# Inverse norms of a two-layer attention block by logarithm, exponential and a Newton step, with a newly searched order of operations

## The chip, the cores and the metric

The kernel runs on one core of one Trainium2 chip. The metric is the device time of one execution in microseconds. Five engines work side by side: TensorE (PE in the profile, its weight loads PEld), VectorE (DVE), ScalarE (ACT), GpSimd (POOL), and SyncE (SP), which here only issues DMAs.

## The reference

Everything is in float32. The input x has 4 sequences of 1024 positions with 256 features. It is normalized (layer norm), and two branches work on the result; their sum and x are the output.

```
xn  = layernorm(x)
out = x + first(xn) + layers(xn)

first(xn):                         # one attention, 16 heads of 64
    h = rms_norm(xn) * gamma
    q, k, v = h @ W_qkv            # window of 64 keys back
    o = softmax(mask(q k^T / 8)) v
    return (o * sigmoid(h @ W_gates + b_gates)) @ W_out

layers(x), twice:                  # 8 heads of 64
    h = shift_token(x)             # half of the features from the position before
    q, k, v = h @ wqkv
    q = q / |q| * q_scale          # l2norm per head
    k = k / |k| * k_scale
    q, k = rotary_xpos(q, k)       # cos, sin and a scale by position
    o = softmax(mask(8 q k^T)) v   # window of 128 keys back
    x = x + o @ wo
    h = layernorm(shift_token(x)) * ln_g + ln_b
    a, g = split(h @ w1 + b1)
    x = x + (a * gelu(g)) @ w2 + b2
```

## The kernel before

The 4096 positions are worked off in 16 blocks of 256 (`TB`), each in two halves of 128 positions (`NT` = 2), one position to a partition. For each block there are three passes: `first_attention`, and `layer` for layers 0 and 1 with `after_attention` behind it (the part from the residual to the gated feed-forward). The first attention of all blocks comes first, and layer 0 starts while its last blocks are still being worked on (`MIX` = 3). A layer's `after_attention` for a block is written down up to two blocks later (`LAG` = 2).

The code does not issue these steps directly. Each step becomes an `Op` of a `Plan`, with the engines that may do it, an estimated duration on each, the buffers it reads and writes, and, for ScalarE, a mode ("exp" or "gelu"; a change of mode makes ScalarE load another table). `Plan.run` then plays the whole program through in time while the kernel is being built. Whenever an engine is free it takes the waiting operation with the lowest score:

```
score = o.due + self.IDLE * (t - at[e]) + (self.TURN[e] if turn else 0.0)
if o.dense and row - self.REFILL * (t - at[e]) + o.dense > self.ROW:
    score += self.CROWD
```

Here `due` is when the operation is due for TensorE's sake, `IDLE` is the price of leaving the engine idle, `TURN` the price of a change of mode, and `CROWD` a price for standing many small matmuls close together. `DEAR` weighs an engine against another where an operation has a choice. `spare` says how many buffers of each kind are held back. The outcome is one list, `plan.order`; `emit` issues it in that order, so each engine's queue and the DMA queues of SP follow it.

TensorE works in two modes: "full" (128x128 weights) for projections, feed-forward and transposes, and "rc" (64x64 weights, four places of the array) for attention scores and sums. Lines that matter below: 791 (first attention's queries and keys), 702 (its values), 825 and 917 (its scores and sums), 952 (its output projection), 1009 (a layer's query, key and value projection), 1150 (its scores), 1242 (its attention sums), 1267 (its output projection), 1437 (the feed-forward's first product, "up"), 1483 and 1497 (its second, "down" and its rest). Line 431 is ScalarE's half of `move`, which copies PSUM to SBUF (or SBUF to SBUF); 433 is VectorE's. Line 500 is the transpose of 32x32 blocks on VectorE behind a DMA round trip through DRAM; 483 and 492 are the DMAs of that round trip.

The place of the change is in `layer`. For each half block, `sq` (line 1043, ScalarE) squares queries and keys, `ss` (line 1050, VectorE) sums them over each head into 16 numbers per position, and `norms` (lines 1056 to 1058, GpSimd) makes the inverse square roots: a maximum with 1e-24, `rsqrt` (line 422, an element-wise power of −0.5 with a tile of exponents, `mhalf`), and a change of sign for the 8 query heads. There are 64 such half blocks (2 layers, 16 blocks, 2 halves). The key half of the result scales the rotated keys (`kn`, line 1119) before they are transposed; the query half comes in later, as a factor in the masked minimum over the scores (`least`, line 1171), whose sign makes the largest score the least. The exponential of line 1185 follows, then the reciprocal of the sums (line 1197) and the weighing on GpSimd (line 1205). Rotation is `rot` (line 1077, GpSimd), `cos` (1093, VectorE) and `add` (1101, either). `rsqrt` is used too for the first attention's statistics and for the layer norm in `after_attention` (`deviation`, lines 1355 to 1366). The gelu is line 1451, its product with the other half lines 1462 and 1467.

Of the kernel before, what the change touches and what calls it, by code (L numbers as in the profile page):

```python
# [8 lines left out]
AF = mybir.ActivationFunctionType  # L9
ALU = mybir.AluOpType  # L10
# [3 lines left out]
P = 128  # L14
# [17 lines left out]
HB = 8  # L32
# [15 lines left out]
LAG = 2  # L48
MIX = 3
BOTH = False  # L50

# [6 lines left out]

# [9 lines left out]
class Op:  # L71
    __slots__ = (
        "us", "fn", "bufs", "mode", "out", "rank", "lat", "left", "ready", "users", "done",
        "start", "end", "eng", "name", "n", "due", "dense",
    )


class Plan:
    LAT = {"PE": 0.25, "DVE": 0.20000000000000004, "ACT": 0.20000000000000004, "POOL": 0.20000000000000004, "SP": 2.0}
    SLACK = {"DVE": 1.1, "POOL": 1.05, "ACT": 1.15}  # L80
    SWITCH = {"PE": 0.1, "ACT": 1.4}
    TURN = {"PE": 10.0, "ACT": 60.0}
    IDLE = 200.0
    LOOK = 150.0
    ROW, REFILL = 640, 300.0
    CROWD = 60.0
    DEAR = {"DVE": 3.0}

# [8 lines left out]

    def op(self, us, fn, r=(), w=(), a=(), mode=None, out=None, lat=None, name="", dense=0):


        o = Op()
        o.us, o.fn, o.mode, o.lat, o.name = us, fn, mode, lat, name
        o.dense = dense
        o.out = out or mode
# [3 lines left out]
        o.users, o.done, o.ready = [], False, 0.0  # L108
        deps = set()
        for b in r:  # L110
# [18 lines left out]
    def run(self):  # L129
        engines = ("PE", "ACT", "DVE", "POOL", "SP")  # L130
        at = dict.fromkeys(engines, 0.0)
        mode = dict.fromkeys(engines)
# [7 lines left out]
        for o in reversed(self.ops):  # L140
            took = min(o.us.values()) + (0.5 if o.lat is None else o.lat)
            o.due = min([o.rank, *(u.due - took for u in o.users)])
        for o in self.ops:
            if not o.left:
                enter(o)
        oldest, out, row = 0, [], 0
# [17 lines left out]
        while len(out) < len(self.ops):  # L164
# [57 lines left out]
            for u in o.users:  # L222
                u.ready = max(u.ready, give)
                u.left -= 1
                if not u.left:
                    enter(u)
            out.append(o)
        self.order = out

    def emit(self):  # L230
        for o in self.order:
            o.fn(o.eng)


@with_exitstack
def layers_kernel(
# [41 lines left out]
        },  # L278
        {"w": (3, 0.05, 20), "g": (1, 0.0, 1), "s": (4, 0.05, 12), "ps": (0, 0.02, 3), "d": (1, 0.0, 1)},
    )  # L280
# [3 lines left out]
    def fixed(shape, name):  # L284
        return Buf(None, const.tile(shape, F32, name=name))
# [87 lines left out]
    load(mask_a.t, mask_a_d, mask_a, eng="ACT")  # L373
    mhalf = fixed([P, 2 * HB], "mhalf")
    op({"POOL": 0.1}, lambda e: nc.gpsimd.memset(mhalf.t, -0.5), w=(mhalf,))
# [39 lines left out]
    def by_feature(b, i, near=False):  # L415


        of = "p (c i a r) -> p i c a r" if near else "p (a c i r) -> p i c a r"
        return b.t[:, : NT * DIM].rearrange(of, a=4, c=NC, i=NT)[:, i]

    def rsqrt(dst, src):
        nc.gpsimd.tensor_tensor(dst, src, mhalf.t[:, : src.shape[1]], ALU.pow)  # L422
# [543 lines left out]
    def layer(l, n, before):  # L966
# [33 lines left out]
        for i in range(NT):  # L1000
# [38 lines left out]
            for m in range(2):  # L1039
# [14 lines left out]
                )  # L1054
            def norms(e, nrm=nrm, rn=rn):
                nc.gpsimd.tensor_scalar_max(nrm.t[:, : 2 * HB], nrm.t[:, : 2 * HB], 1e-24)
                rsqrt(rn.t[:, : 2 * HB], nrm.t[:, : 2 * HB])
                nc.gpsimd.tensor_scalar_mul(rn.t[:, :HB], rn.t[:, :HB], -1.0)

            op({"POOL": 3.5}, norms, r=(mhalf,), w=(nrm, rn), name="rn")  # L1060
            qT = buf("w")
# [497 lines left out]
    plan.run()  # L1559
    plan.emit()  # L1560

def _constants():
# [5 lines left out]
    def half_tiles():  # L1570


        c, r = np.arange(WB)[None, :], p % D
        at = (c >= r) & (c <= r + P)
        first = at & (c >= np.where(p >= D, D, P))
        return np.where(np.stack([at, first], 1), f(0), f(-1e30)).astype(f)

# [15 lines left out]
    cos, sin = np.cos(freqs), np.sin(freqs)  # L1593
    ways = (scale * f(8), f(1) / scale)

# [44 lines left out]
```

## Time and profile before

| | |
|---|---|
| times of three runs | 1695.48, 1693.13, 1694.20 us; median 1694.2 us |
| the profiled execution | 1694.2 us, span 1694.2 us |
| granted TensorE clock | 1.000 |
| busy, share of the span | PE 99%, VectorE 76%, GpSimd 70%, ScalarE 66% |
| instructions | 48683 |
| DMA | 353 MB, mean 208 GB/s |

Busy time is the union of an engine's instructions. Matmuls are pipelined and the profile models their ends, so a busy TensorE need not be at its peak. The page also cuts the span into 40 slices with the busy share in tenths, follows back the chain of work that ended last, and lists groups of instructions by line: busy time, mean duration in ns, idle time of the engine just before them, and what ended it. The list of waits says who waited for whom: total, times, longest.

### The profile page before, as it was taken

The numbers are of one execution on the slowest core, as the hardware profiler recorded it, in microseconds if no ns is written. First come the engines' busy times: TensorE is split into PE (matmuls) and PEld (weight loads), VectorE is DVE, ScalarE is ACT, GpSimd is POOL, SyncE is SP. The second block draws the span as 40 slices with busy tenths as digits, with TensorE's granted clock in tenths as the row PEclk, the third lists the DMA queues.
The fourth block names the chain that finished last, engine by engine and source line by source line (L and its number), as shares of the span: only waits on it lengthen the run. The fifth ranks groups of instructions, "written<-read, shape, count | busy, mean of one in ns | idle before, by whom it ended". The sixth has DMA issues, their size and how long they took to land.

```text
span 1694.2 us, 48683 instructions
## 1 busy us (share of the span) xinstructions
PE 1669.5 (99%) x16454; PEld 1269.0 (75%) x16454; DVE 1288.3 (76%) x4508; ACT 1121.9 (66%) x3417; POOL 1192.5 (70%) x2013
## 2 busy tenths in 40 slices
PE   9999999999999999999999999999999999999998
PEld 7888888888877767777777776677667767777777
DVE  5665655655657788888888878888899888888863
ACT  4665675656657776776676667766677677667763
POOL 4663654644467889888788779887798688887840
PEclk9999999999999999999999999999999999999999
DMA  7885776866567887877778887887778867777760
GB/s 222 237 233 155 224 213 193 228 175 182 167 169 218 227 232 225 222 204 221 215 200 239 236 221 208 248 238 202 201 217 238 242 198 212 213 222 216 203 197 22
DMA packets 487383, 353.16 MB, mean 208 GB/s; under 512 B 167639, under 2 KB 424542, under 8 KB 487134
## 3 DMA queue, kind: packets, MB, share of 16 engines
q1 hardware_dynamic: 486430, 349.86, 72.7%
q8 instruction: 129, 2.11, 0.5%
q14 instruction: 120, 0.98, 0.2%
q10 hardware_dynamic: 704, 0.21, 0.1%
HBM read 168.29 MB, written 143.92 MB: 184 GB/s over the span
## 4 chain that ended last, share of the span: by engine, by line
PE 53%; POOL 3%; DVE 1%; ACT 1%; issue 1%; DMA 1%; SPq 0%; POOLq 0%; DVEq 0%; ACTq 0%
PE ps L1437 17%; PE ps L1009 14%; PE ps L1483 7%; PE ps L1267 6%; PE ps L1242 4%; PE ps L1150 4%; POOL w L1077 1%; PE ps L1497 1%; POOL s L422 1%; POOL w L1205 1%; ACT w L431 1%; DMA w<-d 0%; DMA out_dram<-w 0%; POOL w L1101 0%; DMA sc<-in_L_ffn_k_scale_dram 0%
## 5 line engine op out<-in xcount | busy, mean ns | idle before, releaser
L431 ACT COPY w<-ps 128x512 f32<-128x512 f32 (+3 forms) x624 | 327.7, 585 | 329.7 <-PE ps L791 96.3
L500 DVE STREAM_TRANSPOSE w<-w 128x256 f32<-128x256 f32 (+2 forms) x781 | 450.5, 621 | 95.7 <-DMA w<-d 35.8
L1009 PE MATMUL ps<-w,w 128*128 128x512 f32 x768 | 347.6, 595 | 1.7 <-DVE w L1467 0.7
L880 POOL TENSOR_SCALAR w<-w,s,s 128x128 f32<-128x128 f32 x512 | 227.5, 462 | 146.1 <-DVE s L870 114.0
L1437 PE MATMUL ps<-w,w 128*128 128x256 f32 (+1 forms) x1452 | 312.0, 373 | 1.1 <-ACT w L431 1.1
L1437 PEld LDWEIGHTS ps<-w,w 128*128 128x128 f32 x1452 | 268.3, 190 | 45.5 <-issue 5.9
L1205 POOL TENSOR_SCALAR w<-w,s 128x192 f32<-128x192 f32 (+1 forms) x512 | 230.7, 471 | 91.8 <-DVE s L1197 85.7
L422 POOL TENSOR_TENSOR s<-s,mhalf 128x16 f32<-128x16 f32 (+3 forms) x113 | 228.9, 2025 | 62.7 <-DVE s L643 32.6
L1185 ACT ACTIVATE w<-w,s 128x192 f32<-128x192 f32 (+1 forms) x512 | 223.0, 439 | 48.1 <-DVE w L500 11.2
L1009 PEld LDWEIGHTS ps<-w,w 128*128 128x128 f32 x768 | 144.3, 190 | 147.3 <-issue 127.0
L1077 POOL TENSOR_TENSOR w<-w,w 128x256 f32<-128x256 f32 x256 | 198.2, 780 | 58.9 <-ACT w L431 38.8
L791 PE MATMUL ps<-w,w 128*128 128x256 f32 x1024 | 230.3, 381 | 2.9 <-ACT w L431 1.7
L791 PEld LDWEIGHTS ps<-w,w 128*128 128x128 f32 x1024 | 193.0, 190 | 37.1 <-ACT w L431 3.9
L861 ACT ACTIVATE w<-w,s 128x128 f32<-128x128 f32 x512 | 197.4, 390 | 23.8 <-DVE s L851 11.6
L1171 DVE CUSTOM_DVE_ANT_0 w<-ps,mask_b,s 128x192 f32<-128x192 f32 (+1 forms) x512 | 177.9, 402 | 15.4 <-PE ps L1150 4.9
L1483 PE MATMUL ps<-w,w 128*128 128x256 f32 x640 | 144.8, 380 | 3.6 <-DVE w L1462 3.3
L1093 DVE TENSOR_TENSOR w<-w,w 128x256 f32<-128x256 f32 x256 | 125.8, 537 | 27.4 <-ACT w L431 21.1
L1483 PEld LDWEIGHTS ps<-w,w 128*128 128x128 f32 x640 | 120.9, 190 | 30.7 <-issue 9.9
L1451 ACT ACTIVATE g<-ps,b 128x256 f32<-128x256 f32 (+1 forms) x198 | 86.4, 467 | 84.8 <-PE ps L1437 82.0
L851 DVE CUSTOM_DVE_ANT_0 w<-ps,mask_a 128x128 f32<-128x128 f32 x512 | 111.8, 284 | 28.9 <-PE ps L825 24.4
L1267 PE MATMUL ps<-w,w 128*128 128x256 f32 x512 | 126.6, 390 | 6.7 <-ACT w L431 3.1
L1267 PEld LDWEIGHTS ps<-w,w 128*128 128x128 f32 x512 | 92.7, 189 | 35.7 <-ACT w L431 15.7
(87 smaller groups left out, 2471.2 us busy)
## 6 DMA issues: line engine op xcount, KB each, us to landing
d<-w SPq DMA_DIRECT2D x301, 256.0 KB
w<-d SPq DMA_DIRECT2D x301, 256.0 KB
d<-w SPq DMA_DIRECT2D x224, 192.0 KB
w<-d SPq DMA_DIRECT2D x224, 192.0 KB
w<-w SPq DMA_DIRECT2D x256, 128.0 KB
w<-c SPq DMA_DIRECT2D x81, 256.0 KB
c<-w SPq DMA_DIRECT2D x48, 256.0 KB
w<-in_L_attn_x_dram SPq DMA_DIRECT2D x16, 256.0 KB
```

Of the source, the lines that this page charges most:

```text
L422: nc.gpsimd.tensor_tensor(dst, src, mhalf.t[:, : src.shape[1]], ALU.pow)
L431: nc.scalar.copy(dst(), src())
L500: lambda e, b=b, to=to, at=at, k=k: nc.vector.transpose(to(b), v3(t, 4, m, 32)[:, :, at : at + k]),
L791: nc.tensor.matmul(pq.t[:, j * TB : (j + 1) * TB], W[c].t[:, p % GA * P : (p % GA + 1) * P], hT.t[:, c * TB : (c + 1) * TB], start=(c == 0 ...
L880: nc.gpsimd.tensor_scalar(run(s, u), run(s, u), sm.t[:, at : at + 1], gate.t[:, h : h + 1], ALU.mult, ALU.mult,)
L1009: nc.tensor.matmul(p.t, y.t[:, at : at + P], w["wqkv"][m][c].t[:, :512], start=(c == 0), stop=(c == NC - 1),)
L1077: nc.gpsimd.tensor_tensor(rot.t[:, :512].rearrange("p (h u k r) -> p u k h r", h=2, u=2, k=PB)[:, u], raw[m].t[:, :512].rearrange("p (k h ...
L1185: nc.scalar.activation(v2(ex, 2, (3 - k0) * D)[:, u].rearrange("p (a k r) -> p k a r", k=3 - k0, a=2), v2(s, 2, WB)[:, u, k0 * D :].rearra ...
L1205: nc.gpsimd.tensor_scalar(v2(ex, 2, m)[:, u], v2(ex, 2, m)[:, u], sm.t[:, at : at + 1], 1.0, ALU.mult, ALU.mult,)
L1267: nc.tensor.matmul(pw.t[:, :DIM], v3(oT, 2, 2, P)[:, p % 2, p // 2], v2(w["wo"][p // 2], 2, DIM)[:, p % 2, :], start=(p == 0), stop=(p == ...
L1437: nc.tensor.matmul(pf.t[:, n_ * TB : (n_ + 1) * TB][:, cols], wt, d.t[:, c * TB : (c + 1) * TB][:, cols], start=(c == 0), stop=(c == NC - 1),)
L1483: nc.tensor.matmul(pz.t[:, :DIM], gT[m // 2].t[:, at : at + P], v2(w["w2"][m // 2], 2, DIM)[:, m % 2, :], start=(m == 0), stop=False,)
```

## The change

Three things change. The norms of the layers leave GpSimd's power: the sums are clamped on VectorE or GpSimd, ScalarE takes their logarithm and the exponential of −0.5 times it, and VectorE or GpSimd refines this with one Newton step. The sign of the queries moves into the rotation tables, and that of the mask with it. And the order is another: the planner's prices have other values, 28 ranges of operations have their due times shifted by pseudo-random amounts (`NUDGES`), a matmul operation that follows another on TensorE counts as ready when that one ends, and the table that has both logarithm and exponential is loaded by name whenever ScalarE turns to "exp".

```diff
+NUDGES = [
+    (3500828213, 6053, 6213, 26), (962684833, 7739, 7818, 42), (972045936, 7349, 7406, 6),
+    (83998847, 153, 210, 5), (76883089, 7565, 7620, 20), (3275595751, 4672, 4864, 6),
+    (438986454, 7689, 7721, 90), (1531916726, 5229, 5323, 9), (3939820594, 7664, 7861, 21),
+    (3050749052, 2441, 2480, 24), (971591458, 4443, 4747, 4), (2170321430, 4709, 4906, 24),
+    (3913640632, 4835, 4963, 4), (842596981, 2642, 2828, 12), (814815308, 5466, 5547, 25),
+    (2025033581, 2674, 2735, 11), (352340027, 7429, 7565, 6), (1888537629, 7649, 7682, 18),
+    (3075992983, 7680, 7721, 91), (951854742, 6717, 6777, 9), (159045329, 7340, 7419, 34),
+    (2211461150, 2597, 2649, 15), (1845618598, 3431, 3526, 5), (763246061, 6898, 6987, 12),
+    (3348864259, 7298, 7342, 4), (200214347, 5984, 6059, 6), (1383019642, 2231, 2285, 19),
+    (318795953, 2687, 2722, 9),
+]
+HASTE = 1.2477144070116626
...
+def part(seed, i):
+    x = (seed * 2654435761 + i * 2246822519) & 0xFFFFFFFF
+    x = (x ^ x >> 15) * 2654435761 & 0xFFFFFFFF
+    return (x ^ x >> 13) / 4294967296.0 - 0.5
...
-    TURN = {"PE": 10.0, "ACT": 60.0}
-    IDLE = 200.0
-    LOOK = 150.0
+    TURN = {"PE": 7.841459753622532, "ACT": 17.36077070419636}
+    IDLE = 251.92185968639595
+    LOOK = 158.7882403426324
     ROW, REFILL = 640, 300.0
-    CROWD = 60.0
-    DEAR = {"DVE": 3.0}
+    CROWD = 17.03349668372114
+    DEAR = {"DVE": 1.9317326986533034}
...
+        sway = [0.0] * len(self.ops)
+        for seed, lo, hi, by in NUDGES:
+            for i in range(lo, hi):
+                sway[i] += by * part(seed, i)
         for o in self.ops:
+            o.due = o.due - o.hurry * HASTE + sway[o.n]
...
-                u.ready = max(u.ready, give)
+                u.ready = max(u.ready, o.end if e == "PE" and "PE" in u.us else give)
...
-    def emit(self):
+    def emit(self, load_exp):
+        mode = None
         for o in self.order:
+            if o.eng == "ACT" and o.mode:
+                if o.mode == "exp" and mode != "exp":
+                    load_exp()
+                mode = o.mode
             o.fn(o.eng)
...
-        {"w": (3, 0.05, 20), "g": (1, 0.0, 1), "s": (4, 0.05, 12), "ps": (0, 0.02, 3), "d": (1, 0.0, 1)},
+        {"w": (0.0, 0.07702659706019774, 35.46116717265452), "g": (1.0, 0.0, 1.0), "s": (4.0, 0.05, 12.0), "ps": (0.0, 0.02268601358766725, 3.0), "d": (1.0, 0.0, 1.0)},
...
-    mhalf = fixed([P, 2 * HB], "mhalf")
+    mhalf = fixed([P, 4], "mhalf")
...
-            def norms(e, nrm=nrm, rn=rn):
-                nc.gpsimd.tensor_scalar_max(nrm.t[:, : 2 * HB], nrm.t[:, : 2 * HB], 1e-24)
-                rsqrt(rn.t[:, : 2 * HB], nrm.t[:, : 2 * HB])
-                nc.gpsimd.tensor_scalar_mul(rn.t[:, :HB], rn.t[:, :HB], -1.0)
-
-            op({"POOL": 3.5}, norms, r=(mhalf,), w=(nrm, rn), name="rn")
+            op(
+                {"DVE": 0.16, "POOL": 0.34},
+                lambda e, x=nrm: vec[e].tensor_scalar(
+                    x.t[:, : 2 * HB], x.t[:, : 2 * HB], 1e-24, 1e37, ALU.max, ALU.min
+                ),
+                w=(nrm,), name="rn",
+            )
+
+            def guess(e, nrm=nrm, rn=rn):
+                nc.scalar.activation(rn.t[:, : 2 * HB], nrm.t[:, : 2 * HB], AF.Ln)
+                nc.scalar.activation(rn.t[:, : 2 * HB], rn.t[:, : 2 * HB], AF.Exp, scale=-0.5)
+
+            op({"ACT": 0.4}, guess, r=(nrm,), w=(rn,), mode="exp", name="rn")
+
+            def refine(e, nrm=nrm, rn=rn):
+                y, x = rn.t[:, : 2 * HB], nrm.t[:, : 2 * HB]
+                t = rn.t[:, 2 * HB : 4 * HB]
+                vec[e].tensor_tensor(t, y, y, ALU.mult)
+                if e == "POOL":
+                    vec[e].tensor_tensor(t, x, t, ALU.mult)
+                    vec[e].tensor_scalar(t, t, -0.5, 1.5, ALU.mult, ALU.add)
+                    vec[e].tensor_tensor(y, t, y, ALU.mult)
+                    return
+                vec[e].scalar_tensor_tensor(t, x, -0.5, t, ALU.mult, ALU.mult)
+                vec[e].scalar_tensor_tensor(y, t, 1.5, y, ALU.add, ALU.mult)
+
+            op({"DVE": 0.5, "POOL": 1.2}, refine, r=(nrm,), w=(rn,), name="rn")
...
-    plan.emit()
+    plan.emit(lambda: nc.scalar.preload_act_table_set("natural_log_exp_and_others"))
...
-        return np.where(np.stack([at, first], 1), f(0), f(-1e30)).astype(f)
+        return np.where(np.stack([at, first], 1), f(0), f(1e30)).astype(f)
...
-    ways = (scale * f(8), f(1) / scale)
+    ways = (scale * f(-8), f(1) / scale)
```

Not shown are two added fields of an operation, `hurry` and `after`, which no operation of the kernel sets.

More of the change, by code (lines that the diff above doesn't have):

```diff
@@ L73 @@
         "us", "fn", "bufs", "mode", "out", "rank", "lat", "left", "ready", "users", "done",
-        "start", "end", "eng", "name", "n", "due", "dense",
+        "start", "end", "eng", "name", "n", "due", "dense", "hurry",
     )
@@ L96, in buf, with op @@
         return Buf(kind)
-    def op(self, us, fn, r=(), w=(), a=(), mode=None, out=None, lat=None, name="", dense=0):
+    def op(self, us, fn, r=(), w=(), a=(), mode=None, out=None, lat=None, name="", dense=0, hurry=0.0, after=()):
         o = Op()
         o.us, o.fn, o.mode, o.lat, o.name = us, fn, mode, lat, name
-        o.dense = dense
+        o.dense, o.hurry = dense, hurry
         o.out = out or mode
@@ L108, in op @@
         o.users, o.done, o.ready = [], False, 0.0
-        deps = set()
+        deps = set(after)
         for b in r:
@@ L419, in by_feature @@
         return b.t[:, : NT * DIM].rearrange(of, a=4, c=NC, i=NT)[:, i]
+    vec = {"DVE": nc.vector, "POOL": nc.gpsimd}
     def rsqrt(dst, src):
```

## The prediction

> **What bounds the kernel now.** I read the head of the page first (busy time of each engine, then the 40 slices).
>
> ```profile
> PE 1669.5 (99%) x16454; PEld 1269.0 (75%) x16454; DVE 1288.3 (76%) x4508; ACT 1121.9 (66%) x3417; POOL 1192.5 (70%) x2013
> ...
> PE   9999999999999999999999999999999999999998
> ...
> POOL 4663654644467889888788779887798688887840
> PEclk9999999999999999999999999999999999999999
> ```
>
> TensorE (PE) is busy in every slice, at a granted clock of 1.000; only 1694.2 − 1669.5 = 24.7 us of the span are without a matmul. GpSimd (POOL), from which the change takes work, is at 8 to 9 tenths from slice 12 on (the layers), but PE is full there too. The change touches no matmul, so what it can win is only time that PE loses. The windows by stage and PE's own waits say where that lies:
>
> ```profile
> 740.00:1000.00 260.00, 259.30 (x2282) 189.33 (x2275) 221.07 (x660) 183.42 (x496) 211.66 (x319) 1.00 0.77 218
> ...
> 1650.00:1694.20 44.20, 37.77 (x288) 32.76 (x286) 14.65 (x39) 13.34 (x32) 3.11 (x6) 1.00 0.09 27
> ```
> ```profile
> PE ps L1483 <- DVE w L1462: 3.3, 3, 1.2
> PE ps L1267 <- ACT w L431: 3.1, 6, 1.1
> PE ps L791 <- ACT w L431: 1.7, 5, 0.4
> ```
>
> In the first the columns are length, then busy time of PE, weight loads, VectorE (DVE), ScalarE (ACT), POOL. In mid-layers PE lacks 0.7 us of 260; in the last 44.2 us it lacks 6.4. PE never waits for POOL directly by more than 0.5 us; its waits are for ScalarE's evictions and VectorE's gelu products.
>
> A busy PE is not a PE at its peak, since matmul ends are modelled, so I took the steady price from the chain of work that ended last:
>
> ```profile
> 708.77 5.15 PE ps L1009 x12
> 719.08 9.50 PE ps L1437 x44
> ```
>
> 5.15/12 = 0.429 us for a 512-wide matmul, 9.50/44 = 0.216 for a 256-wide one. Stepping through all matmul starts of the trace and taking each step against the median of its kind: 252 steps are 0.02 to 0.15 us too long, 24.1 us together (about 0.095 each, nearly all where PE passes between 128x128 and 64x64 matmuls, 217 passages); 36 are longer than that, 27.1 us together. Of these 27.1, 2.9 lie in the first 20 us, 17.7 between 20 and 1600 us, and 6.5 in five stops after 1600 us. So PE's removable loss is about 27 us and its unremovable one about 24, unless the order needs fewer passages. That is the frame: at best near 1694.2 − 24 = 1670; there is no such floor on the slow side. The profiled execution took 1694.2 us, its span is the same, and it is the median of the runs shown, so no conversion is needed.
>
> **The change part by part.**
>
> Norms. These rows go or are the nearest to what comes:
>
> ```profile
> L422 POOL TENSOR_TENSOR s<-s,mhalf 128x16 f32<-128x16 f32 x64 | 187.7, 2932 | 5.3
> L1056 POOL TENSOR_SCALAR s<-s 128x16 f32<-128x16 f32 x64 | 20.8, 326 | 10.0 <-DVE s L1050 5.0
> L1058 POOL TENSOR_SCALAR s<-s 128x8 f32<-128x8 f32 x64 | 18.5, 290 | 5.9
> L756 ACT ACTIVATE s<-s 128x32 f32<-128x32 f32 x16 | 3.6, 225 | 1.3 <-DVE s L752 1.3
> L761 DVE TENSOR_SCALAR s<-s 128x32 f32<-128x32 f32 x16 | 3.9, 244 | 3.6 <-ACT s L756 3.5
> L653 DVE SCALAR_TENSOR_TENSOR s<-s 128x2 f32<-128x2 f32 x16 | 2.4, 150 | 4.4 <-POOL s L422 4.4
> ```
>
> POOL loses 187.7 + 20.8 + 18.5 = 227.0 us: 1192.5 becomes 965.5. ScalarE gains 64 x 2 activations of 128x16; the 128x32 row bounds one at 0.225, so 28.8 us, 1121.9 to 1150.7. Clamp and Newton step are four instructions on VectorE, between 0.150 and 0.244 each: 0.6 to 1.0 us a norm, 38 to 62 us, 1288.3 to at most 1350; or, where the planner chooses POOL, five there at 0.3 each, at most 96 us. I take VectorE with 0.7 x 64 = 45 us. In 740 to 1000 us VectorE has 221 of 260 us (85%); 45 us over the 1100 us of the layers adds 4 points: 89%, still below PE. As a chain a norm falls from 0.33 + 2.93 + 0.29 = 3.55 us on one engine to about 0.2 + 0.45 + 0.5 plus two hand-overs of some 0.15 (VectorE's end at 5.98 to POOL's start at 6.13 in the first norm): 1.5 us. Who waits for it is few: the waits for line 422 are 5.5 us in total of the keys' scaling (line 1119) 1.3 of an eviction and 0.8 of the minima (line 1171), none of it on PE. What the freed POOL is worth is then not 227 but a part of the 17.7 us of mid-kernel stops: its weighing (L1205) feeds the transposes without which the attention matmuls can't go. The chain that ended last has 3% on POOL, 51 us, of which PE shows as lost only what is in the 17.7. Bounds 0 and 17.7; I take a third, 6 us, since most of the stops name ScalarE and VectorE, not POOL.
>
> The added waits. Each engine runs its list in the emitted order, so an early logarithm on ScalarE holds the PSUM evictions (L431) queued behind it, for which PE waits already; VectorE's Newton step waits for ScalarE in turn and holds gelu products behind it. These are up to 64 stops each of 0.15 to 0.3 us if badly placed, 0 to 19 us of engine time, and cost PE only where its next operand is the one held; I take 0 and keep the upper end for the range.
>
> Tables. The pair counts as an "exp" operation, so it must fall in an exp stretch of ScalarE or open one.
>
> ```profile
> L1451 ACT ACT_TABLE_LOAD x31 | 39.8, 1283 | 0.5
> L1185 ACT ACT_TABLE_LOAD x30 | 38.5, 1283 | 16.0 <-PE ps L1267 9.3 <-DVE s L1171 5.6 <-issue 0.8
> ```
>
> There are 61 switches now, 78 us. The preloaded set, by its name, serves both functions, so the pair itself needs none; but the planner's price of a switch falls from 60 to 17, so more is likely: bounds 61 and 61 + 128 loads (each norm its own stretch in and out), +164 us, ScalarE 1315 us or 78%. I take 90 (+37 us), hidden below PE. Here a rule speaks against the change: the Trainium skill (ScalarE: Activation LUTs, What ACT_TABLE_LOAD costs) puts a switch at about 2.66 us, a drain of 1.38 included. The trace shows the load at 1240.69 after an activation that ended at 1240.66, and the next activation at 1241.98, so 1.3 us in all; by the page's figure the worst case would be 340 us and ScalarE at 88%.
>
> Order. Ten of the 28 ranges in NUDGES lie at or above operation 7298 of 7861, so they reorder the end. Five stops with 6.5 us lie there (the largest: 1.5 us at 1686.5, before the last "down"). The last stop is a dependency chain of gelu, product, matmul with little else left; I take half, 3 us, of bounds 0 and 6.5. Passages between matmul shapes: TURN for PE falls from 10 to 7.8, which allows more; the nudges may save some; 0.095 us each, 20 either way is 2 us; I take 0. CROWD falls from 60 to 17: dense runs of small matmuls may stand closer; the one visible stop of this sort (505 us, 0.8 + 0.9 us) bounds one at 1.7; I take 0.
>
> With one answer, nothing: the sign in the tables and masks (same instructions, other constants), the shorter mhalf, the PE-to-PE readiness in the planner (PE is in order anyway), `hurry` and `after` (no operation passes them).
>
> Sum: 1694.2 − 6 − 3 = 1685.2; I say 1685.
>
> **The rivals.**
> *The order finds nearly everything.* The 27.1 us fall to the first 2.9 plus a few: 1694.2 − 20 = 1674. For it: every engine but PE has room. Against: 36 separate stops with a dozen different partners.
> *PE is full, nothing moves.* Mid-layers lack 0.7 us of 260; new stops replace old ones: 1691 to 1697, say 1693.
> *ScalarE's tables cost PE.* Norms break the gelu runs. PE makes a gelu's input every 8 x 0.216 = 1.73 us, the gelu takes 0.47, so a break of two loads (2.57 us) comes out 2.57 − 1.26 = 1.3 us late; VectorE's product is late by it, and PE stops at the "down" matmuls (L1483), where its largest wait is today. If 13 of the 64 norms do this without other PE work ready: +17 us less 3 at the end, 1708. From 7 on it eats the gain. For it: the cheaper switch in the planner. Against: LAG keeps two blocks' work at hand, and mid-layers hide 61 loads today.
> *It does not do what it says:* if logarithm and exponential each reload, 128 loads more; by the case above, also over 1700.
>
> The Trainium skill (Perfetto Trace Analysis, Identifying the Most-Contended Engine) says to judge TensorE by weight-load busy time, not by matmul busy time. That would read 75% and promise room; here a 0.190 us load (the mean of line 1437's group) stands under each 0.216 us matmul, so the steps above, not the 75%, measure the room.
>
> **How the numbers follow.** Forecast (gain of 4 to 15 us) 0.50; order finds nearly everything 0.12; nothing moves 0.18; tables or another added wait, 0.20 (tables 0.17, the reloads 0.03). A difference under 0.2% (3.4 us) can't be told from none. Faster: 0.50 + 0.12 = 0.62; same 0.18; slower 0.20. Range 1671 to 1702: below it is under one in ten of everything (PE's floor is at 1670), above it about half of the slow cases.
>
> **What would show it.** In the changed profile: no 128x16 operation of 2.9 us on POOL, POOL near 965 to 1060 us; ScalarE with 128 more activations and some 90 loads; PE's matmul time by line unchanged, its idle time under 20 us; the last 44 us with PE over 39 us busy. Wrong if: ScalarE's loads exceed 130 with "L1483 <- DVE" above 10 us (tables), or PE's idle time stays at 25 with other partners (nothing moves), or stops in 20 to 1600 us grow beyond 18 us.

## The result and the profile after

| | before | changed |
|---|---|---|
| median | 1694.84 us (4 runs, 1693.13 to 1696.02) | 1710.49 us (4 runs, 1707.38 to 1713.10) |
| the profiled execution | 1694.20 us, span 1694.2 us | 1711.93 us, span 1709.0 us |
| ratio to before | | 1.0087, interval 1.0075 to 1.0099 |

The change makes the kernel slower by 0.9%, about 15.6 us. The forecast was a gain of 9. In the changed kernel the lines stand 29 to 52 further down: 825, 917, 1009, 1150, 1267 and 1437 of before are 856, 948, 1040, 1202, 1319 and 1489; 431 is 462; 1093 is 1145; 1462 is 1514 and 1497 is 1549. New are 1088 (the clamp), 1095 and 1096 (logarithm, exponential), 1103 to 1110 (Newton step) and 1612 (the table load).

The head of the changed kernel's page, and two of the 40 slices' rows:

```profile
span 1709.0 us, 48793 instructions
PE 1672.7 (98%) x16454; PEld 1272.3 (74%) x16454; DVE 1347.9 (79%) x4646; ACT 1147.0 (67%) x3541; POOL 1027.3 (60%) x1972
...
DVE  5855656565558879999889988998989888898973
...
POOL 3745555554457666767567666765776676666730
```

The work went where it was meant to go: GpSimd 1192.5 to 1027.3 us, ScalarE 1121.9 to 1147.0, VectorE 1288.3 to 1347.9. TensorE's matmuls are the same 16454, but 1709.0 − 1672.7 = 36.3 us are without one, where before it was 24.7. Steady prices are unchanged; in the chain that ended last (start, duration, line, matmuls) 12 of the 512-wide matmuls and 44 of the 256-wide ones still take

```profile
1389.87 5.15 PE ps L1040 x12
...
1456.86 9.50 PE ps L1489 x44
```

So TensorE does the same work at the same pace and stops more. The windows by stage (length, then busy time of PE, weight loads, VectorE, ScalarE, GpSimd, clock, DMA share, GB/s) say where; first the changed kernel,

```profile
0.00:500.00 500.00, 487.29 (x5510) 402.69 (x5511) 302.32 (x1476) 302.73 (x1130) 257.74 (x581) 1.00 0.69 199
500.00:1600.00 1100.00, 1080.16 (x9969) 783.00 (x9968) 977.26 (x2959) 783.10 (x2248) 733.23 (x1323) 1.00 0.76 216
...
1665.00:1709.00 44.00, 40.29 (x302) 35.04 (x300) 14.58 (x41) 13.89 (x34) 3.10 (x6) 1.00 0.12 37
```

and the kernel before in the same two long windows:

```profile
0.00:500.00 500.00, 493.65 (x5649) 406.20 (x5650) 301.33 (x1487) 302.71 (x1141) 260.56 (x587) 1.00 0.71 201
500.00:1600.00 1100.00, 1089.98 (x10003) 791.54 (x10002) 937.31 (x2865) 770.11 (x2145) 901.02 (x1372) 1.00 0.77 220
```

In the first 500 us TensorE lacks 12.7 us where it lacked 6.4, and gets through 139 fewer matmuls. That is the first attention: the first matmul of a layer starts at 498.6 us, so no norm that the change rewrites is at work there. In the layers it lacks 19.8 where it lacked 10.0. In the last 44 us it lacks 3.7 where it lacked 6.4. Besides, from 10.8 to 14.1 us the profiled execution of the changed kernel had a granted clock of 0.50 (0.91 over the first 20 us, where the kernel before had 1.00), which costs some 1.7 us of longer steps.

TensorE's waits in the whole span (total, times, longest) name two partners that the kernel before had little of or not at all:

```profile
PE ps L856 <- issue: 6.7, 9, 1.5
PE ps L1319 <- DVE w L1561: 5.6, 6, 1.6
PE ps L948 <- issue: 4.0, 5, 1.4
PE ps L1040 <- DVE s L1223: 2.2, 4, 0.9
...
PE ps L1319 <- DVE s L1088: 1.5, 1, 1.5
```

In the kernel before, the line for the second was

```profile
PE ps L1267 <- DVE w L1509: 1.4, 1, 1.4
```

**The first partner is "issue": nothing that the profile shows as a wait.** In the first 500 us the changed kernel has

```profile
PE ps L856 <- issue: 5.8, 8, 1.5
PE ps L948 <- issue: 3.8, 4, 1.4
```

and the kernel before has no such line there; its list begins

```profile
PE ps L791 <- ACT w L431: 1.7, 5, 0.4
PE ps L446 <- DVE w L662: 1.3, 1, 1.3
PE ps L320 <- DVE still L316: 1.2, 1, 1.2
```

One such place in the changed kernel's timeline (start, duration; in brackets the idle time before):

```profile
129.04 4.00 PE L948 MATMUL ps<-w,w 64*64 64x128 f32 x189
134.28 0.33 PE L948 MATMUL ps<-w,w 64*64 64x64 f32 x3 [1.24 <-issue]
134.41 3.71 PE L856 MATMUL ps<-w,w 64*64 64x128 f32 x124
138.94 0.44 PE L856 MATMUL ps<-w,w 64*64 64x128 f32 x4 [0.83 <-issue]
139.31 5.88 PE L983 MATMUL ps<-w,w 128*128 128x256 f32 x26
```

Here 192 small matmuls of the sums are followed at once by 128 of the scores: 320 matmuls, 640 instructions with their weight loads. The changed kernel has 12 such long runs, nine of 640 instructions and three of 576; the kernel before has none over 384. In its trace the 192 matmuls are followed by a 128x128 product:

```profile
128.65 4.39 PE L917 MATMUL ps<-w,w 64*64 64x128 f32 x192
132.97 7.17 PE L952 MATMUL ps<-w,w 128*128 128x256 f32 x32
```

Instructions are fetched over DMA queues of their own; the DMA view of 131.5 to 133 us has one such packet:

```profile
q8 instruction: 1, 0.02, 4.6%
```

The page has 129 packets on this queue with 2.11 MB, 16 KB each; TensorE's 2 x 16454 instructions in 129 packets are 255 a packet, so I take the queue for TensorE's. The packet seen here is on the way from 131.68 to 132.79 us; TensorE runs dry just after 132.8 and goes on at 134.28, 1.49 us after the packet landed. At all twelve "issue" stops of the first 500 us TensorE goes on 1.25 to 1.58 us after a packet has landed. The kernel before has two "issue" stops in its whole span, 2.5 and 5.4 us after a landing. From the start of the packet's transfer, TensorE ran on for 0.6 to 2.3 us before the twelve stops; transfer and lag together took 2.2 to 2.9 us, and the stop is the difference. Three of the eleven long runs that begin before 500 us have no stop. This reading is inferred from times in the traces; what triggers a fetch is not in them.

**The second partner is VectorE.** Line 1561 takes the result of a feed-forward's second product out of PSUM. The next output projection (1319) waits for it, by the code for a PSUM buffer that line 1561 sets free. At the largest of these stops the timeline of all engines reads (start, duration)

```profile
1173.72 2.35 DVE L1145 TENSOR_TENSOR w<-w,w 128x256 f32<-128x256 f32 x2
1173.78 1.48 PE L1202 MATMUL ps<-w,w 64*64 64x192 f32 x32
...
1174.34 1.45 POOL L1153 TENSOR_TENSOR w<-w,w 128x512 f32<-128x512 f32 x1
1175.99 0.74 DVE L1561 TENSOR_TENSOR w<-ps,w 128x256 f32<-128x256 f32 x2
...
1176.88 1.32 PE L1319 MATMUL ps<-w,w 128*128 128x256 f32 x5 [1.62 <-DVE w L1561]
```

VectorE is in two cosine products that take 2.35 us where the planner reckons 0.68 times 1.1 for the pair, so line 1561 starts late and TensorE stops for 1.62 us after 1.48 us of scores. The groups behind it (busy time, mean ns | idle before):

```profile
L1145 DVE TENSOR_TENSOR w<-w,w 128x256 f32<-128x256 f32 x256 | 146.0, 613 | 45.4 <-ACT w L462 41.6 <-PE ps L1294 2.2 <-PE ps L948 0.5
...
L1110 DVE SCALAR_TENSOR_TENSOR s<-s 128x16 f32<-128x16 f32 x33 | 12.1, 366 | 1.3
...
L1103 DVE TENSOR_TENSOR s<-s 128x16 f32<-128x16 f32 x33 | 9.6, 290 | 0.4 <-ACT s L1096 0.2
L1109 DVE SCALAR_TENSOR_TENSOR s<-s,s 128x16 f32<-128x16 f32 x33 | 9.5, 288 | 2.1
L1088 DVE TENSOR_SCALAR s<-s 128x16 f32<-128x16 f32 x26 | 9.4, 361 | 0.1
```

A Newton step on VectorE is 0.29 + 0.29 + 0.37 = 0.94 us, for the planner 0.5; a clamp is 0.36, for the planner 0.16; two cosine products are 1.23 in the mean, for the planner 0.68 (it multiplies each of its prices for VectorE by 1.1). The plan is drawn by such prices, so it fills VectorE more than it thinks.

To compare runs I took each step between matmul starts against one fixed price for its kind (429, 323, 229, 216 and 112 ns for 512, 384, 272, 256 and 128 columns, and the steady prices of the small kinds) and added up what exceeds it: **TensorE's lost time**. It counts the passages between matmul shapes too, so it is somewhat more than the prediction's 51.2 us of longer steps.

| us lost | first 500 us | after 500 us | sum | span |
|---|---|---|---|---|
| before | 21.1 | 39.4 | 60.6 | 1694.2 |
| changed | 31.5 | 43.5 | 75.0 | 1709.0 |

The sums differ by 14.4 us, the spans by 14.8: this is the whole loss. After 1600 us 7.9 became 2.4, so the three parts are +10.4 in the first attention, +9.6 in the layers, −5.5 at the end. Of the +10.4, the half-clock stretch at 10.8 us is 1.7; the "issue" stops in the long runs are 9.6, and the rest of that stage loses a little less than before.

### The profile page after: what moved, and what is told of

Read it like the earlier page. It is cut to its first block, busy times and chain, and to the rows that moved or that the text cites. A ratio compares the mean times of both kernels' runs of the same rounds, so it can differ in the third digit from the quotient of the medians.

```text
span 1709.0 us, 48793 instructions
## 1 busy us (share of the span) xinstructions
PE 1672.7 (98%) x16454; PEld 1272.3 (74%) x16454; DVE 1347.9 (79%) x4646; ACT 1147.0 (67%) x3541; POOL 1027.3 (60%) x1972
## 3 DMA queue, kind: packets, MB, share of 16 engines
q8 instruction: 129, 2.11, 0.5%
## 5 line engine op out<-in xcount | busy, mean ns | idle before, releaser
L462 ACT COPY w<-ps 128x512 f32<-128x512 f32 (+2 forms) x646 | 335.1, 584 | 317.0 <-PE ps L822 91.2
L1257 POOL TENSOR_SCALAR w<-w,s 128x192 f32<-128x192 f32 (+1 forms) x512 | 235.2, 479 | 112.6 <-DVE s L1249 99.9
L1129 POOL TENSOR_TENSOR w<-w,w 128x256 f32<-128x256 f32 x256 | 205.2, 806 | 126.3 <-ACT w L462 99.3
L1145 DVE TENSOR_TENSOR w<-w,w 128x256 f32<-128x256 f32 x256 | 146.0, 613 | 45.4 <-ACT w L462 41.6
L882 DVE CUSTOM_DVE_ANT_0 w<-ps,mask_a 128x128 f32<-128x128 f32 x512 | 112.9, 285 | 43.5 <-PE ps L856 36.0
L1153 POOL TENSOR_TENSOR w<-w,w 128x512 f32<-128x512 f32 x87 | 111.1, 1281 | 19.0 <-DVE w L1145 13.3
```

Of the source, the lines that this page charges most:

```text
L462: nc.scalar.copy(dst(), src())
L1129: nc.gpsimd.tensor_tensor(rot.t[:, :512].rearrange("p (h u k r) -> p u k h r", h=2, u=2, k=PB)[:, u], raw[m].t[:, :512].rearrange("p (k h ...
L1257: nc.gpsimd.tensor_scalar(v2(ex, 2, m)[:, u], v2(ex, 2, m)[:, u], sm.t[:, at : at + 1], 1.0, ALU.mult, ALU.mult,)
```

## The experiments

The first theory was that the new order alone costs the time; its rival, that the new norms alone do. Later came the two in the sections above: instruction fetches that the planner doesn't know, and VectorE prices that are too low. All ratios are to the kernel before on the same chip, and lost times are from the profiled executions. The chips differ a little (the kernel before took 1694.8 to 1696.8 us on them), so a difference between medians of two chips is good to some 2 us, and where the two disagree the ratios decide.

**e1_norms_only.** The changed kernel with the order's settings of before, so that the planner makes its own plan for the new norms.

```diff
-NUDGES = [...28 ranges...]
+NUDGES = []
-TURN = {"PE": 7.84, "ACT": 17.36}; IDLE = 251.9; LOOK = 158.8; CROWD = 17.03; DEAR = {"DVE": 1.93}
+TURN = {"PE": 10.0, "ACT": 60.0}; IDLE = 200.0; LOOK = 150.0; CROWD = 60.0; DEAR = {"DVE": 3.0}
...
-u.ready = max(u.ready, o.end if e == "PE" and "PE" in u.us else give)
+u.ready = max(u.ready, give)
```

> The changed kernel with the order made as before (old prices, old spare buffers, no shifts of due times, old readiness): the norms alone. Theory A, the order is to blame (long unbroken runs of 64x64 matmuls outrun TensorE's instruction fetches, and output projections come too soon behind the scores): about 1690, between 1683 and 1698, with TensorE's stops inside lines 856 and 948 under 3 us together. Theory B, the norms are to blame (added ScalarE and VectorE steps hold evictions and the freeing of PSUM banks): 1703 to 1713, as the changed kernel.

Measured: 1724.6 us, 1.0166 (1.0149 to 1.0183). Lost 21.1 us in the first 500 us, as before, and 69.6 after it.

**e2_order_only.** The kernel before, with power and signs, under all the new settings; the shifts are mapped to the same operations.

```diff
+NUDGES, part, sway as in the change (an old "rn" counts as three operations)
-TURN, IDLE, LOOK, CROWD, DEAR, spare, readiness of before
+those of the change
```

> The kernel before, its norms on GpSimd as they were, with the new prices, spare buffers, readiness and shifts of due times (each operation takes the shift of its place in the new list): the order alone. Theory A: 1703 to 1715, with some 10 us of stops inside the first attention's small matmuls. Theory B: 1685 to 1696.

Measured: 1719.7 us, 1.0140 (1.0125 to 1.0155); lost 28.7 and 51.8. Both are slower than either theory allowed, and each half alone is slower than both together. The halves don't add; each of them has a plan of its own. But the 28.7 in the first 500 us come with the order, without the norms: this plan too has the 12 long runs.

**e3_crowd0_before.** The kernel before with one price changed.

```diff
-    CROWD = 60.0
+    CROWD = 0.0
```

> The kernel before with one constant changed, the price for standing small matmuls close together, from 60 to 0: its order then has twelve unbroken runs of 640 small-matmul instructions in the first attention, as the changed kernel's has, and fewer passages (199 for 217). Theory A: stops without a releaser inside the first attention's small matmuls grow from under 1 to 8 to 14 us, each ending 1.3 to 1.5 us after an instruction fetch has landed; 1699 to 1710. Theory B, or a theory in which fewer passages are a gain: 1690 to 1696.

Measured: 1706.9 us, 1.0066 (1.0048 to 1.0084); lost 31.3 and 38.1. Its plan has 12 long runs in the first attention (nine of 640 instructions, three of 576), as has that of the changed kernel, where the plan of before has none, and TensorE's waits begin as in the changed kernel:

```profile
PE ps L825 <- issue: 4.5, 6, 1.5
PE ps L917 <- issue: 2.4, 3, 1.1
```

One price brings the long runs and most of the first +10 us, with no more lost in the layers (38.1 against 39.4). In the first 500 us 6.6 us are "issue" stops, each 1.40 to 1.59 us after a packet has landed; some 3 us of the 10.2 lie in two half-clock stretches (at 10 and 75 us).

**e4_no_newton.** The changed kernel's order held; the clamp and the Newton step issue nothing. It leaves out the refinement, so the norms are the raw exponential.

```diff
-                lambda e, x=nrm: vec[e].tensor_scalar(...1e-24, 1e37, ALU.max, ALU.min),
+                lambda e: None,
...
-            op({"DVE": 0.5, "POOL": 1.2}, refine, ...
+            op({"DVE": 0.5, "POOL": 1.2}, lambda e: None, ...
```

> The changed kernel, order held, without the clamp and the Newton step (the inverse norms stay the tables' own): VectorE and GpSimd lose some 40 and 40 us of work. Theory A: the first 500 us unchanged, the layers a little better where output projections wait for VectorE, 1704 to 1709. Theory B: most of the loss goes, 1692 to 1700.

Measured: 1704.8 us, 1.0053 (1.0038 to 1.0068), 0.34% or 5.7 us less than the changed kernel. The clamp and the Newton step, on VectorE and GpSimd together, cost that much in this order; some 9 us of the loss are there without them.

**e5_new_norms_old_order and e6_old_norms_new_order.** The order of before held, its three GpSimd instructions replaced by clamp, logarithm, exponential and Newton step at the same place; and the reverse, the changed order held with maximum and power on GpSimd at the Newton step's place.

```diff
-                nc.gpsimd.tensor_scalar_max(...); rsqrt(...); nc.gpsimd.tensor_scalar_mul(...)
+                nc.vector.tensor_scalar(x, x, 1e-24, 1e37, ALU.max, ALU.min)
+                nc.scalar.activation(y, x, AF.Ln); nc.scalar.activation(y, y, AF.Exp, scale=-0.5)
+                three VectorE instructions of the Newton step
```

The cut leaves out that e5 also takes over the signs in tables and masks, and loads ScalarE's table where it is not at "exp".

> The kernel before, its order held to the operation; only where GpSimd's three instructions of a norm stood now stand the clamp and the Newton step on VectorE and the pair on ScalarE (a table load where ScalarE is not at exp). Theory A, a new order costs whatever the norms are: 1690 to 1700, since few wait for a norm. Theory B, the norms' instructions themselves hold ScalarE's and VectorE's queues: 1705 to 1725.

> The changed kernel, its order held to the operation; the clamp and the pair issue nothing, and the norm is GpSimd's maximum and power at the Newton step's place. Theory A: 1706 to 1716, the first 500 us as in the changed kernel, the layers worse where the power comes late. Theory B: 1692 to 1700.

Measured: 1757.5 us, 1.0361 (1.0336 to 1.0385), and 1811.7 us, 1.0688 (1.0660 to 1.0715), both far above what either theory allowed. In e5 TensorE's longest wait is that of a feed-forward's first product for VectorE, and so it is in e6:

```profile
PE ps L1449 <- DVE w L1479: 18.9, 13, 3.1
```
```profile
PE ps L1475 <- DVE w L1505: 25.9, 16, 3.5
```

In both, an order held while the durations changed under it lost far more than a new plan. In e6 some 27 us of the loss lie in stretches of half clock (its granted clock is 0.983 in the mean). The first 500 us follow the order (lost 22.5 with that of before, 31.1 with the changed one), whichever norms run later.

**e7_rerolled_a and e8_rerolled_b.** The kernel before, with every due time shifted by up to 1 us at random, twice.

```diff
         for o in self.ops:
+            o.due += 2.0 * part(11, o.n)     # 12 in the second
```

> The kernel before, only with every operation's due time shifted at random by up to 1 us either way, so that the planner makes another order of the same kind (243 passages for 217, no more long runs). Theory A, the order before was a good draw and any new plan loses on the chip: 1698 to 1712. A theory in which the plan's details do not matter: 1693 to 1697.

> The same with other random shifts (237 passages). Theory A: 1698 to 1712, and not the same time as the first; details do not matter: 1693 to 1697.

Measured: 1712.5 us, 1.0095 (1.0077 to 1.0113), and 1708.5 us, 1.0068 (1.0050 to 1.0086); lost after 500 us 53.6 and 48.5 instead of 39.4. With the same work and the same prices these two other draws of the plan cost 12 and 17 us. So the plan of before looks like a good draw, and a change that makes the planner draw again may start that far behind. It need not: e3 is another plan in the layers too (VectorE has 4486 instructions for 4508) and loses no more there. And whether the random shift itself makes a plan worse, no run tells.

**e9_split_order.** The changed kernel, with the prices of before in force only while the first attention works.

```diff
+            early = oldest < first - self.EARLIER     # first: a layer's first operation; EARLIER = 0
+            for k, v in (old if early else new).items():
+                setattr(self, k, v)
```

> The changed kernel, planned with the prices of before as long as only the first attention is at work and with the new ones after it: no run of 640 small-matmul instructions is left (221 passages). If the long runs are worth what the first 500 us show (8 to 10 us) and the layers' part of the order keeps its quality: 1698 to 1704. If every new plan of the layers loses as the two redrawn ones did: 1706 to 1716, with the first 500 us back at 21 to 24 us of lost TensorE time either way (31 in the changed kernel).

Measured: 1710.5 us, 1.0077 (1.0062 to 1.0092). The long runs are gone and the first 500 us lose 23.7 instead of 31.5, but the layers were drawn anew and lose 53.1 instead of 43.5. The first 8 us came back and were lost again; the total shows nothing, the stages do.

**e10, e11, e12: a planner that knows both.** The new norms, with a stop of 1.2 us in the planner's clock where its count of a run of small matmuls passes `ROW` = 640, and with VectorE's and GpSimd's prices as the trace has them (clamp, Newton step, cosine, and in the same way the addition, the scaling of keys and the rotation). Prices and shifts of the order were then searched at random from three seeds against the planner's own end, which now contains the stops. The planner's count is not the trace's: it takes a score operation for 128 where the trace has 64 instructions, so its 640 are 320 in the trace, less than the 384 that the kernel before runs without a stop. The model is thus stricter than the trace.

```diff
+    STOP = 1.2
...
+                if row > self.ROW:
+                    t, row = t + self.STOP, 0.0
...
-                {"DVE": 0.16, "POOL": 0.34},                 # clamp
+                {"DVE": 0.33, "POOL": 0.34},
-            op({"DVE": 0.5, "POOL": 1.2}, refine, ...
+            op({"DVE": 0.86, "POOL": 1.0}, refine, ...
-                op({"DVE": 0.68}, times_cos, ...
+                op({"DVE": 1.02}, times_cos, ...
...
-    CROWD = 17.03349668372114
+    CROWD = 101.0505171899954                                # e11; found by the search
```

> The new norms with a planner that knows what the traces showed: a run past ROW stops TensorE for 1.2 us, and the two-input operations of VectorE and the norm's steps cost what they were measured at (cosine 1.02, key scaling 0.95, sum 0.76, clamp 0.33, Newton 0.86 us); prices and 13 shifts of due times found by a new search from the old settings. If the change lost because the search was led by these wrong prices: 1680 to 1695, no stops without a releaser in the first attention, under 55 us lost. If the norms themselves are the loss: above 1700.

> The same planner and the same norms, another search, from the new settings (32 shifts): 1680 to 1695 by the wrong-prices theory, above 1700 if the norms are the loss.

> A third search of the same kind, from the old settings (10 shifts; more of the norms' steps on GpSimd: 108 of 128): 1682 to 1697 by the wrong-prices theory, above 1700 if the norms are the loss.

| | us | ratio to before | lost, first 500 us | after |
|---|---|---|---|---|
| e10 | 1684.3 | 0.9920 (0.9905 to 0.9935) | 22.9 | 26.1 |
| e11 | 1681.9 | 0.9907 (0.9892 to 0.9921) | 20.8 | 24.4 |
| e12 | 1691.5 | 0.9970 (0.9959 to 0.9982) | 22.2 | 31.2 |

All three beat both kernels; e11 is 28.6 us ahead of the changed one (1.8% by the ratios, 30 us), and no run in the three plans is over 320 instructions. Its page, its first wait and a window of mid-layers:

```profile
PE 1666.6 (99%) x16454; PEld 1268.6 (76%) x16454; DVE 1352.3 (81%) x4685; ACT 1116.0 (66%) x3456; POOL 1039.7 (62%) x2028
```
```profile
PE ps L502 <- DVE w L718: 1.8, 1, 1.8
```
```profile
700.00:1000.00 300.00, 300.00 (x2662) 218.91 (x2661) 262.71 (x796) 219.95 (x606) 205.26 (x377) 1.00 0.79 221
```

VectorE is as busy as in the changed kernel (1352 against 1348 us), yet TensorE has no gap in the 300 us; the changed kernel has

```profile
700.00:1000.00 300.00, 297.36 (x2577) 215.63 (x2579) 271.28 (x789) 213.97 (x586) 198.84 (x351) 1.00 0.77 218
```

So the amount of VectorE's work over the whole span does not decide; where it stands must count, though in this window e11's VectorE has less to do as well (263 against 271 us).

**e13, e14, e15.** What was open: which of the two corrections matters, and whether the new norms do. The same search from e11's seed with only the prices corrected (e13), with only the stop (e14), and the norms of before with both (e15).

```diff
-    STOP = 1.2                                   # e13 against e11: without it and its two lines
...
-            op({"DVE": 0.86, "POOL": 1.0}, refine, ...     # e14 against e11: the old prices, with STOP
+            op({"DVE": 0.5, "POOL": 1.2}, refine, ...
...
-            op({"POOL": 3.5}, norms, ...         # e15: kept as before, with STOP and the measured prices
```

> The new norms, the planner with the measured prices but without the stop for long runs, searched as long as and from the same start as the second searched version (seed 3, CROWD 60 at the start). The search went back to CROWD 19 and to twelve runs of 640 small-matmul instructions. If the missing stop term is what cost: 8 to 12 us above the second searched version (1681.9), 1689 to 1696, with some 9 us of stops without a releaser in the first 500 us. If only the prices matter: 1678 to 1686.

> The new norms, the planner with the stop for long runs but with the prices of the changed kernel (cosine 0.68, key scaling 0.68, sum 0.61, clamp 0.16, Newton 0.5 us), same start and length of search; no long runs, 213 passages. If the wrong prices of VectorE's work are what cost in the layers: 1694 to 1706, with over 35 us lost after 500 us and waits of lines 1319 and 1489 for VectorE. If only the long runs matter: 1680 to 1688.

> The kernel before with its power on GpSimd, planner with stop and measured prices, searched from the old settings, a shorter search (2400 against 3000 s; of three searches that ended within 1 us in the plan, one). What the norms are worth with an order as good: if the new norms are a gain of their own, this is 4 to 12 us above the best searched version with them, 1686 to 1694; if they are worth nothing, 1680 to 1686; above 1694 the power itself costs more than any wait of the profile before shows.

| | us | ratio to before | lost, first 500 us | after |
|---|---|---|---|---|
| e13 prices only | 1695.9 | 1.0007 (0.9998 to 1.0016) | 30.6 | 29.9 |
| e14 stop only | 1710.7 | 1.0083 (1.0063 to 1.0103) | 28.8 | 48.0 |
| e15 old norms | 1696.8 | 1.0007 (0.9997 to 1.0016) | 22.9 | 36.9 |

Without the stop the search itself lowered CROWD from 60 to 19, its plan has 12 long runs again, and TensorE's waits begin

```profile
PE ps L881 <- issue: 6.9, 8, 1.4
PE ps L973 <- issue: 1.6, 3, 1.0
```

It loses 9.8 us more than e11 in the first 500 us (8.5 us are such stops, 1.6 a half-clock stretch at 9.4 us) and is 14 us slower. Without the measured prices TensorE's waits begin with VectorE and the output projection, as in the changed kernel:

```profile
PE ps L1345 <- DVE w L1587: 5.2, 6, 2.0
PE ps L848 <- ACT w L488: 3.6, 7, 2.0
PE ps L1345 <- DVE s L1129: 3.5, 1, 3.5
```

That is 29 us behind e11, more than expected. Some 7 us of it lie in four half-clock stretches of the profiled execution, and the one run of e14 at a full clock took 1704.6. Its first 500 us lose 28.8 though no long run is there: line 848 waits 4.5 us for ScalarE, one "issue" stop is 2.0 us, and two of the half-clock stretches, 3.4 us, lie there. So long runs are not the only way to lose 8 us in that stage. With the old norms the search ends where the kernel before stands, 12 to 15 us behind e10 and e11, 5 behind e12, above the whole range that was expected. These three are one search each, and e10 to e12 differ among themselves by 9.6 us, so a difference between two searches is good to some 10 us. The 29 us of the prices, GpSimd's included, are beyond that, also without the 7. The 14 us of the stop are not by themselves, but 9.8 of them lie in the first stage and at the stops named. The new norms' own gain, 5 to 17 us by medians and ratios, is likely and not settled.

## Why the prediction was wrong

- **The first step that failed is CROWD**: "dense runs of small matmuls may stand closer; the one visible stop of this sort (505 us, 0.8 + 0.9 us) bounds one at 1.7; I take 0". The edit was seen, but the stop it went by is of another sort: in the waits of the kernel before, the two stops (at 505 and 507 us) are

```profile
PE ps L825 <- POOL w L1101: 0.5, 1, 0.5
PE ps L952 <- DVE s L851: 0.7, 1, 0.7
```

Those are waits for GpSimd and VectorE, and the last instruction packets had landed 0.6 and 2.4 us before TensorE went on, not 1.25 to 1.58. The profile before shows no stop like the changed kernel's, so the term stood at nothing without a row for it. That 1.7 is near what one run lost (2.07 us of idle time in the place shown, 9.6 us over eleven runs) is luck. What came is 12 long runs, one per block for most of the first attention: +10.4 us, 9.6 of it in such stops. e3 shows by one number that CROWD brings them. Their number could have been reckoned ahead: 192 + 128 matmuls a block, 16 blocks.
- **The second is the layers**: "I take a third, 6 us", and for the added waits "I take 0". It came to +9.6 us, where 6 were to be won. The upper bound of 19 us for the added waits held; the value was at the wrong end. e4 puts 5.7 us on clamp and Newton step in that order. The rest, and the gain that did not come, are likely the draw of the plan, for which e7 and e8 show 12 and 17 us; no run shows it for this plan. The prediction treated the plan before as typical and the new one as equal or better; the range of a redraw was no term in its sum. Put together: 1694.2 + 10.4 + 9.6 − 5.5 = 1708.7, the measured span within 0.3 us.
- **The sums of engine time were right and did not decide.** GpSimd between 965 and 1060: 1027. VectorE at most 1350: 1348, in the layers 977 of 1100 us or 89%, as reckoned. But of the +60 us the norms are 31 (Newton) and 9.4 (clamp) on just 33 and 26 of 64 half blocks, where 45 were reckoned for all 64; the largest other shifts are scaling of keys that moved over (60 to 90 instructions, +21.6) and dearer cosine products (+19.5), less additions that moved to GpSimd (−16.3). A VectorE norm costs 0.94 + 0.36 = 1.30 us, above the upper end of "0.6 to 1.0 us a norm".
- **The tables were wrong in count, right in effect.** About 90 loads were expected; there are 30 by name and 30 at the gelu, together 60 where there were 61:

```profile
L1612 ACT ACT_TABLE_LOAD x30 | 38.5, 1283 | 3.2 <-issue 2.7
L1503 ACT ACT_TABLE_LOAD x30 | 38.5, 1283 | 0.5
```

- The rival on tables named 1708, close to the result, but its mechanism did not come: 60 loads, and TensorE's idle time before the "down" matmuls (1483 of before, now 1535) is 0.9 us in all, none of it on VectorE. The number was right by chance. The loss came from VectorE and from TensorE's own instructions.
- **Right**: the end. Half of 6.5 us, 3, was taken; 7.9 became 2.4, and TensorE is busy for 40.3 of the last 44 us. Passages between shapes were taken as equal at 0.095 us each; there are 173 instead of 217, some 4 us, and they are in the sum above already. "Stops in 20 to 1600 us grow beyond 18 us" was the mark given for wrong, and it is what happened.
- The frame, "at best near 1670", was not refuted: e11 comes to 1679.2 of span with the same norms.

## What to carry to other kernels

When an order is drawn by a planner, price a redraw as a term of its own: here two plans of the same work with shifts of 1 us cost 12 and 17 us, about as much as the edit's whole loss, so a change that re-plans must be compared with a plan searched as well for the other side. Give the planner each cost the trace shows before searching with it, since a search goes where the model is blind: here long runs of small matmuls and VectorE's short instructions, and with both priced the same norms went from 0.9% slower to 0.3 to 0.9% faster in three searches. And where a cost per event is seen once, look up what that event waited for, and multiply it by the number of such events that the edit allows, before taking it as nothing.

## What the hardware showed beyond this

- TensorE can outrun its own instructions: in the changed kernel 8 of the 11 long runs of small matmuls before 500 us stop once or twice, 0.3 to 1.5 us each, and TensorE goes on 1.25 to 1.58 us after a packet of 16 KB has landed. In e13 the eleven such stops have 1.25 to 1.56 us. The profile calls this "issue", and names no engine.
- VectorE's two-input work has a neighbour. I counted the products that stand beside one GpSimd operation for 70% or more of their time. In the kernel before, a cosine product of 128x256 took 409 ns beside GpSimd's power (32 of them), 416 with GpSimd idle, 468 beside its TENSOR_SCALAR and 743 beside its TENSOR_TENSOR (70); in the changed kernel 411, 448 and 795 (idle, TENSOR_SCALAR, and 118 beside TENSOR_TENSOR). The power was slow but no disturbance; in the changed kernel, without it, GpSimd's two-input work meets VectorE's more often, and the mean product went from 537 to 613 ns. The Trainium skill (GPSIMD Engine Reference, Specifications) says that the two engines share SBUF interfaces and that VectorE's instructions with two SBUF inputs contend; these rows agree, with a factor of 1.9 (795 over 411) between TENSOR_TENSOR and an idle GpSimd.
